# A decoder layer on one core: two more products of the MLP gates by a second Strassen level, and the context codes moved to the Mamba layer

## The chip, the cores and the metric

The kernel runs on one core of one Trainium2 chip. The metric is the device time in microseconds of one execution. Its engines are TensorE (PE), VectorE (DVE), ScalarE (ACT), GpSimd (POOL) and SyncE (SP, which here only issues transfers). Each takes its instructions in the order of the built program (which the language's scheduler settles, except where the source ties one behind another), and waits at an instruction until the semaphores that it needs have come.

## The reference

A decoder layer on x (2 x 512 tokens of 1024 numbers, float32) in three parts, each added to x:

```python
x = x + block(layernorm(x))          # Mamba-2 mixer and a gated MLP (silu(h @ gate.T) * (h @ up.T) @ down.T, 3584 wide)
q1 = fake_quant(layernorm(x)); q2 = fake_quant(ctx)     # round to 0..255 codes; ctx is 2 x 1024 x 1024
x = x + q1 @ q2
W = base + mean(abs(w - base)) * sign(w - base)         # for w1, w3 (gate, up) and w2 (down), 3584 x 1024 each
x = x + silu(h @ W1.T) * (h @ W3.T) @ W2.T              # FFN, h = layernorm(x)
```

So the FFN needs the signs of three weight differences and the mean of their absolute values, and the second part needs the codes of ctx, before either begins. The kernel makes both ahead of time, beside other work.

## The kernel before

The large products use Strassen's method in Winograd's form: seven block products in place of eight, with sums of blocks ahead and behind. The stages stand in this order on PE: the Mamba layer's projections and scan (to about 375 us), its output product, the MLP's gates, the MLP's `down` product with the quantized product between its steps, the FFN's gates, the FFN's `down`.

The function `gates` does both gate stages, name `m` for the MLP and `f` for the FFN. It loops over 14 groups of 256 rows of the gate and the up matrix, taken together. A group's seven block products are made so:

- products 1 and 2, which only appear as their sum, in `O12`. In the MLP (`two=False`), and in each stage for the groups begun early, `first_two` (L319) multiplies them plainly: 16 matmuls of 512 columns (L328), and an eviction by ACT after each four (L332). In the FFN (`two=True`) `second_level` (L763) makes them by a second level of seven products of 256 columns each (four matmuls each, L770), with left sums by `outer_left`, right sums `B12` made once by `second_level_right`, and five sums out of PSUM on DVE.
- products 6 and 7 by `second_level` in both stages (in the names the first letter is the stage, then n, the group and the bank: `mn5a` is bank a of MLP group 5; the second level of products 1 and 2 has m in place of n: `fm4a`).
- products 5, 4 and 3 plainly (`one`, L845), banks c, d and c again.

`second_level` uses bank b twice: of its seven small products the second (6) and the fifth (7) go into the same bank, and between them DVE reads it: `add(u2, p1, ps["b"])`, where p1 is a copy of bank a by ACT. `add` and `sub` are lines L187 and L190. Then come SiLU on ACT and a product on DVE (L903, L905), sums of hidden blocks (`hidden_blocks`), sums of the next group's weights (`left`), and sums of the down weights (`down_blocks`). Eight PSUM banks change sides between groups. `turn`, the sum of `O67`, is where a group's run of DVE sums begins.

Beside the gates of the MLP runs the class `Diffs` (L1101), a step at three places of each group (`side`): 34 steps in all, for w1 and w3 of each group and w2 of the last six. A step's parts stand on two engines in order: on ACT a sign into `sg` (L1147) and an absolute sum (L1148); on POOL the store of the signs (L1121), the loads of the next raw weights and base (`sw`, `smean_w`, L1116), and the subtraction (L1131). All ACT instructions of the stage are chained in the written order by `on_act`, so a sign that waits for POOL holds the evictions behind it. `sw`, `smean_w` and `sg` have two places each. At the steps in `rows`, one in each of groups 1 to 8, the place of the base is loaded with 256 rows of ctx after the subtraction (L1135); ACT (L159), DVE (L162) and ACT (L165) turn them into codes, and POOL stores them in `c2d`.

The last products of a group that are done late (`finished`, the c sum, SiLU and product of slot 3, and the sums and the store of `h`) stand in `later` in the MLP: they are issued in the next group, after two of the four steps of `first_two`.

The other half of w2 has been done in the Mamba layer by `SecondDiffs` (L343): 16 halves of 128x1024, a step at copies and activations of the projections (`at`), the subtraction on POOL (L378), sign and absolute sum on ACT (L371, L372), loads on SP (L361), stores on ACT's queue (L373).

Of the kernel before, what the change touches and what calls it, by code (L numbers as in the profile page):

```python
# [38 lines left out]
def decoder(ctx, tc, a, out):  # L39
# [273 lines left out]
    POOLS = dict(t8=1, w=2, w1=2, raw=2, ap=1, hp=1, o1=1, o12=2, o67=1, px=2, s23=1, s4=2, y12=1, y67=1, b4=2, t4=1)  # L313
# [29 lines left out]
    class SecondDiffs:  # L343

        count = 2 * W2_EARLY
# [15 lines left out]
        def step(self, at):  # L363
# [3 lines left out]
            if n:  # L367
                i, hs = self.halves(n - 1)
                w, sg = self.raw[(n - 1) % 2], self.sg[(n - 1) % 2]
                with tc.issue_after(at):  # L370
                    nc.scalar.activation(sg, w, AF.Sign)  # L371
                    nc.scalar.activation(w, w, AF.Abs, accum_out=sums[:, 2, n - 1 : n])  # L372
                nc.scalar.dma_start(signs[2][i][:, hs], sg)  # L373
            if n + 1 < self.count:
                self.load(n + 1)
            if n < self.count:
# [4 lines left out]
                )  # L381
            self.n += 1
# [380 lines left out]
    def second_level(name, banks, p1, A, B, O, between=lambda: None):  # L763
# [13 lines left out]
        on_act(lambda: nc.scalar.copy(p1, ps["a"]))  # L777
        mm("b", 6)
# [13 lines left out]
    def gates(name, act, acts, g, pl, weights, down_weight, begun, ex, two, side):  # L792
# [4 lines left out]

        act_last[:] = [] if two else [None]
# [4 lines left out]
        with g:  # L803
# [6 lines left out]
            def outer_left(i, gw, uw):  # L810

                y = pl["y12"].tile([P, 4, 2, 2, P], F32, tag="y", name=f"{name}y12_{i}")
                gv, uv = (w[:, :, :P].rearrange("p (q k) c -> p q k c", q=2) for w in (gw, uw))
                return second_level_left(gv, uv, *(y[:, j] for j in range(4)))
# [20 lines left out]
            for i in range(NG):  # L835
# [17 lines left out]
                elif not two:  # L853
                    O12, steps = first_two(name, act, pl, i, *coming[0], X)
                    for n, step in enumerate(steps):
                        if n == 2:
                            late.pop()()
                            begin = last_on(mybir.EngineType.DVE)
                        step()
                else:  # L860
                    O12 = pl["o12"].tile([P, 2, 2, L], F32, tag="o", name=f"{name}o12_{i}")
                    p1 = pl["px"].tile([P, 2, Q], F32, tag="p", name=f"{name}p12_{i}")
                    second_level(f"{name}m{i}", X, p1, A12, B12, O12)
                    add(O12[:, 1], O12[:, 0], O12[:, 1])
                if i == 0:
                    c, d = one("c", 5), one("d", 4)
                p1 = pl["px"].tile([P, 2, Q], F32, tag="p", name=f"{name}p67_{i}")
                O67 = pl["o67"].tile([P, 2, 2, L], F32, tag="o", name=f"{name}o67_{i}")
                second_level(f"{name}n{i}", Y, p1, A67, B67, O67, side or (lambda: None))
# [12 lines left out]
                if not last:  # L882
                    with tc.issue_after(turn):
                        if two and i + 1 not in begun:
                            A12 = outer_left(i + 1, *coming[0])
                        A, A67 = left(i + 1, *coming[0])
                if two and i == 0:
# [4 lines left out]
                if two and not last:  # L892
                    w2.append(down_weight(i + 1, stored))
                b, sums_to, store = w2.pop(0)
                with tc.issue_after(turn if two or not last else begin):
                    down_blocks(b, sums_to())
                store(dram[1][i])
                if not two and not last:
# [8 lines left out]
                def finished(i=i, c=c, O67=O67, h=h, last=last, product=product):  # L907
# [3 lines left out]
                    if side and not last:  # L911
                        side()
                    if last:
                        nc.sync.dma_start(dram[0][i][:, :3, :], h[:, :3, :])
                    hidden_blocks(h)
                    if last:
                        nc.sync.dma_start(dram[0][i][:, 3:, :], h[:, 3:, :])
                        return None
                    return nc.sync.dma_start(dram[0][i], h).ins
# [3 lines left out]
                if two or last:  # L923
                    stored = finished()
                else:
                    side()

                    def later(finished=finished):
                        nonlocal stored
                        stored = finished()  # L930

                    late.append(later)
# [149 lines left out]
    sgp = g.enter_context(tiles_waited(name="sgp", bufs=2))  # L1082
    pl.update(open_pools(g, "m", ("ap", "t8", "hp")))
# [4 lines left out]
    ex = halves(places[0]) + halves(places[1])  # L1088
    pl["px"] = Room(*(ex[3][:, k : k + 2 * Q].rearrange("p (a b) -> p a b", a=2) for k in (0, 2 * Q)))
    pl["o67"] = Room(places[2].rearrange("p (a b c) -> p a b c", a=2, b=2))  # L1090
    pl["y67"] = Room(places[3][:, : 3 * 4 * P].rearrange("p (a b c d) -> p a b c d", a=3, b=2, c=2))
# [8 lines left out]

    class Diffs:  # L1101
        todo = [(i, j) for i in range(NG) for j in range(3) if j < 2 or i >= W2_EARLY]
        rows = {3 + 3 * n: divmod(n, 4) for n in range(2 * TPB)}
# [6 lines left out]
        def load(self, n):  # L1110
            i, j = self.todo[n]
            self.raw[n] = []
            for tag, x in zip(("raw", "base"), FFN[j]):
                tl = pl["raw"].tile([P, KC * GW], F32, tag=tag, name=f"s{x}{i}")
                self.raw[n].append(tl)
# [7 lines left out]
        def subtract(self):  # L1123
            n = self.n
            if not n:
                self.load(0)
            self.store()
            if n + 1 < len(self.todo):
                self.load(n + 1)
            w, v = self.raw[n]  # L1130
            self.on_pool(lambda: nc.gpsimd.tensor_tensor(w, w, v, ALU.subtract))  # L1131
            if n in self.rows:
                b, i = self.rows[n]
                src = a["ctx"][b, i * 2 * P : (i + 1) * 2 * P, :].rearrange("(k p) n -> p k n", p=P)
                self.on_pool(lambda: nc.gpsimd.dma_start(v.rearrange("p (k n) -> p k n", k=2), src))  # L1135

        def step(self):
# [3 lines left out]
            w, v = self.raw.pop(self.n)  # L1141
            coded = self.rows.get(self.n)
            if coded:
                on_act(lambda: code_relu(v, v, inv["x2"], quant["x2_zp"]))
                code_round(v)
# [4 lines left out]
            if coded:  # L1150
                b, i = coded
# [287 lines left out]
```

## Time and profile before

| | |
|---|---|
| median of three runs | 2427.69 us (2424.99 to 2438.13) |
| the profiled execution | 2427.8 us, its span from first to last instruction 2425.9 us |
| mean granted TensorE clock | 0.994 |
| PE busy | 2371.1 us |
| DVE busy | 1537.4 us |
| ACT busy | 614.9 us |
| POOL busy | 413.7 us |
| MLP gates, groups 2 to 13, by PE's timeline | 566.76 to 1136.5 us |
| POOL subtractions in the MLP (L1131) | 34, 4.6 us median, 15.0 the longest |

The profile is of one execution. Its page gives the busy time of each engine, the waits, the chain of work that ended last and the costliest groups of instructions; a line number is that of the source below, and out<-in are the program's names of what is written and read. A matmul of 512 float32 columns counts as two records on PE. A timeline line gives start and duration in us, engine, line, operation, shapes, and in brackets how long the engine had been idle and what released it. A window gives busy time of each engine between two times, then the granted clock, the busy share of the DMA engines and GB/s.

### The profile page before, as it was taken

The numbers are of one execution on the slowest core, as the hardware profiler recorded it, in microseconds if no ns is written. First come the engines' busy times: TensorE is split into PE (matmuls) and PEld (weight loads), VectorE is DVE, ScalarE is ACT, GpSimd is POOL, SyncE is SP. The second block draws the span as 40 slices with busy tenths as digits, with TensorE's granted clock in tenths as the row PEclk, the third lists the DMA queues.
The fourth block names the chain that finished last, engine by engine and source line by source line (L and its number), as shares of the span: only waits on it lengthen the run. The fifth ranks groups of instructions, "written<-read, shape, count | busy, mean of one in ns | idle before, by whom it ended". The sixth has DMA issues, their size and how long they took to land.

```text
span 2425.9 us, 22738 instructions
## 1 busy us (share of the span) xinstructions
PE 2371.1 (98%) x8452; PEld 1543.4 (64%) x8452; DVE 1537.4 (63%) x2278; ACT 614.9 (25%) x784; POOL 413.7 (17%) x296
## 2 busy tenths in 40 slices
PE   7999999999999999999999999999999999999999
PEld 5445444455555555556888775667667667688888
DVE  4757677476555665665555756686776766765554
ACT  3234250334444443311000325222222222100000
POOL 1124211253554354200000011000000000000000
PEclk8999999999999999999999999999999999999999
DMA  4242241668888789756764481677577576786652
GB/s 149 96 155 88 96 147 70 199 224 330 338 356 354 304 353 374 273 190 252 247 182 140 134 238 50 180 195 213 152 199 211 152 199 196 235 261 188 196 170 65
DMA packets 182351, 494.45 MB, mean 204 GB/s; under 512 B 21216, under 2 KB 125664, under 8 KB 151264
## 3 DMA queue, kind: packets, MB, share of 16 engines
q1 hardware_dynamic: 153056, 326.26, 38.6%
q0 software_dynamic: 26880, 162.54, 22.2%
q10 hardware_dynamic: 2304, 4.20, 0.5%
q8 instruction: 67, 1.10, 0.2%
q14 instruction: 44, 0.36, 0.0%
HBM read 349.26 MB, written 145.75 MB: 204 GB/s over the span
## 4 chain that ended last, share of the span: by engine, by line
PE 75%; DMA 9%; POOL 5%; issue 3%; DVE 3%; ACT 3%; SPq 1%; POOLq 0%; ACTq 0%; DVEq 0%
DMA smean_w<-in_mean_w 4%; POOL sw L1131 4%; PE op L664 3%; PE ma L328 3%; DMA smean_w<-in_ctx 2%; SPq L959 1%; ACT sg L1147 1%; DMA m4b<-mwd 1%; PE fa L328 1%; PE dps L440 1%; PE xa L1259 1%; PE y L584 1%; ACT smean_w L159 1%; PE f1c L845 1%; PE f0c L845 1%
## 5 line engine op out<-in xcount | busy, mean ns | idle before, releaser
L1131 POOL TENSOR_TENSOR sw<-sw,smean_w 128x2048 f32<-128x2048 f32 x34 | 190.7, 5609 | 22.5 <-DMA smean_w<-in_mean_w 22.2
L1340 POOL DMA_DIRECT2D fw<-in_mean_w x42 | 36.5, 868 | 530.1 <-ACT fw L1339 479.6
L328 PE MATMUL ma<-h2T,gate_w 128*128 128x512 f32 x224 | 101.4, 595 | 8.9 <-ACT mo L332 8.9
L328 PE MATMUL ma<-h2T,up_w 128*128 128x512 f32 x224 | 102.2, 599 | 0.0
L1339 ACT ACTIVATE fw<-fpl,coeff 128x2048 f32<-128x2048 bf16 x38 | 76.2, 2005 | 91.5 <-DMA fpl<-sign 18.6
L1147 ACT ACTIVATE sg<-sw 128x2048 bf16<-128x2048 f32 x34 | 64.8, 1905 | 114.5 <-POOL sw L1131 114.5
L378 POOL TENSOR_TENSOR raw<-raw,base 128x1024 f32<-128x1024 f32 x16 | 49.9, 3116 | 191.1 <-ACT p00c L520 59.7
L328 PEld LDWEIGHTS ma<-h2T,gate_w 128*128 128x128 f32 x224 | 41.8, 190 | 61.9 <-issue 48.3
L328 PEld LDWEIGHTS ma<-h2T,up_w 128*128 128x128 f32 x224 | 43.1, 193 | 53.9 <-issue 53.9
L905 DVE TENSOR_TENSOR mh<-mpl 128x512 f32<-128x512 f32 x28 | 25.5, 911 | 80.4 <-ACT mpl L903 80.0
L903 ACT ACTIVATE fo<-fo 128x512 f32<-128x512 f32 x56 | 35.0, 626 | 137.5 <-DVE fo L187 137.5
L1148 ACT ACTIVATE sw<-sw 128x2048 f32<-128x2048 f32 x34 | 65.0, 1911 | 1.1
L664 PE MATMUL op<-wout,mz 128*128 128x512 f32 x128 | 56.6, 592 | 0.0
L1121 POOL DMA_DIRECT2D sign<-sg x34 | 19.5, 572 | 199.5 <-ACT sg L1147 199.5
L91 POOL TENSOR_TENSOR q_r<-q_e,mhalf 128x1 f32<-128x1 f32 x8 | 7.0, 876 | 249.9 <-DVE q_e L87 236.9
L332 ACT COPY mo<-ma 128x512 f32<-128x512 f32 x56 | 30.7, 579 | 72.7 <-PE ma L328 66.4
L664 PEld LDWEIGHTS op<-wout,mz 128*128 128x128 f32 x128 | 23.9, 190 | 27.7 <-issue 27.3
L190 DVE TENSOR_TENSOR mh<-mh 128x512 f32<-128x512 f32 x42 | 37.4, 891 | 1.4
L190 DVE TENSOR_TENSOR down<-down 128x512 f32<-128x512 f32 x56 | 38.1, 681 | 0.1
L905 DVE TENSOR_TENSOR fh<-fo 128x512 f32<-128x512 f32 x56 | 36.3, 684 | 1.6
L610 POOL TENSOR_TENSOR mz<-mz,ys 128x512 f32<-128x512 f32 x16 | 20.7, 1293 | 75.0 <-DVE ys L607 43.5
L159 ACT ACTIVATE smean_w<-smean_w,x_zp,inv_x 128x2048 f32<-128x2048 f32 x8 | 16.8, 2094 | 64.9 <-DMA smean_w<-in_ctx 64.9
(2078 smaller groups left out, 5628.6 us busy)
## 6 DMA issues: line engine op xcount, KB each, us to landing
fw<-in_mean_w POOLq DMA_DIRECT2D x42, 1024.0 KB, 13.6
sw<-in_w POOLq DMA_DIRECT2D x34, 1024.0 KB, 9.4
smean_w<-in_mean_w POOLq DMA_DIRECT2D x34, 1024.0 KB, 11.8
mwd<-down SPq DMA_DIRECT2D x14, 1792.0 KB, 10.6
mhd<-mh SPq DMA_DIRECT2D x13, 1792.0 KB, 8.0
fhd<-fh SPq DMA_DIRECT2D x13, 1792.0 KB, 8.1
fpl<-sign SPq DMA_DIRECT2D x38, 512.0 KB, 8.8
sign<-sg POOLq DMA_DIRECT2D x34, 512.0 KB, 6.5
```

Of the source, the lines that this page charges most:

```text
L159: return nc.scalar.activation(v, src, AF.Relu, bias=bias, scale=scale)
L190: nc.vector.tensor_tensor(out_, x, y, ALU.subtract)
L328: nc.tensor.matmul(ps[x], w[:, 4 * p + k, :P], act[0][:, 4 * p + k, :], start=not p and k == 0, stop=k == 3, skip_group_check=p > 0,)
L378: sub_ = nc.gpsimd.tensor_tensor(w, w, self.base[n % 2], ALU.subtract).ins
L664: nc.tensor.matmul(ps, A[p][:, k, t * P : t * P + P], B[p][:, k, :], start=(k == 0), stop=(k == 3))
L845: nc.tensor.matmul(into[x][j], A[j][p][:, k, :], B[p][:, k, :], start=not onto and k == 0, stop=k == 3, skip_group_check=onto,)
L905: nc.vector.tensor_tensor(h[:, slot, :], o[:, 0], o[:, 1], ALU.mult)
L1131: self.on_pool(lambda: nc.gpsimd.tensor_tensor(w, w, v, ALU.subtract))
L1147: on_act(lambda: nc.scalar.activation(sg, w, AF.Sign))
L1148: on_act(lambda: nc.scalar.activation(w, w, AF.Abs, accum_out=sums[:, j, 2 * i : 2 * i + 1]))
L1339: nc.scalar.activation(dst, src, AF.Identity, scale=coeff[:, j : j + 1])
L1340: nc.gpsimd.dma_start(dst, a[base][i].rearrange("p a b -> p (a b)"), accum_op=ALU.add)
```

## The change

- In the MLP, groups 2 to 13 make products 1 and 2 by `second_level`, as the FFN does; groups 0 and 1 still use `first_two`. The right sums `B12` are made in group 1 into a new tile `mex`, and the left sums of the next group after `left`. Their places are a new `y12` and a quarter of a spilled place (`y12_`).
- `finished` and `put` (sums and store of `h`) are separate: with `second_level`, `finished` is issued after the copy of bank a (`copied`), and `put` after the whole product.
- `Diffs` no longer loads or codes ctx. The base has one place in place of two and is loaded after the subtraction, where before it was loaded ahead of it; the signs have one place in place of two.
- `SecondDiffs` codes ctx: after a half's subtraction SP loads 128 rows of ctx into the place of the base, and the next step makes their codes (ACT, DVE, ACT) and stores them from ACT's queue, 16 times.

The diff, cut to its core:

```diff
...
             last["pe"] = last_on(mybir.EngineType.PE)
-    POOLS = dict(t8=1, w=2, w1=2, raw=2, ap=1, hp=1, o1=1, o12=2, o67=1, px=2, s23=1, s4=2, y12=1, y67=1, b4=2, t4=1)
+    POOLS = dict(t8=1, w=2, w1=2, raw=2, ap=1, hp=1, o1=1, o12=2, o67=1, px=2, s23=1, s4=2, y12=1, y67=1, ex=1, b4=2, t4=1)
     def open_pools(g, name, names, **kw):
...
                 i, hs = self.halves(n - 1)
-                w, sg = self.raw[(n - 1) % 2], self.sg[(n - 1) % 2]
+                w, v = self.raw[(n - 1) % 2], self.base[(n - 1) % 2]
+                sg, c16 = self.sg
+                b, k = divmod(n - 1, KC)
                 with tc.issue_after(at):
                     nc.scalar.activation(sg, w, AF.Sign)
-                    nc.scalar.activation(w, w, AF.Abs, accum_out=sums[:, 2, n - 1 : n])
+                    code_relu(v, v, inv["x2"], quant["x2_zp"])
+                code_round(v)
+                nc.scalar.activation(w, w, AF.Abs, accum_out=sums[:, 2, n - 1 : n])
                 nc.scalar.dma_start(signs[2][i][:, hs], sg)
+                code_out(c16, v)
+                nc.scalar.dma_start(c2d[b][:, k, :], c16)
             if n + 1 < self.count:
...
                 )
+                b, k = divmod(n, KC)
+                nc.sync.dma_start(self.base[n % 2], a["ctx"][b, k * P : (k + 1) * P, :])
             self.n += 1
...
         on_act(lambda: nc.scalar.copy(p1, ps["a"]))
+        copied()
         mm("b", 6)
...
             def outer_left(i, gw, uw):
-                y = pl["y12"].tile([P, 4, 2, 2, P], F32, tag="y", name=f"{name}y12_{i}")
                 gv, uv = (w[:, :, :P].rearrange("p (q k) c -> p q k c", q=2) for w in (gw, uw))
+                y = pl["y12"].tile([P, 2 if side else 4, 2, 2, P], F32, tag="y", name=f"{name}y12_{i}")
+                if side:
+                    s4 = pl["y12_"].tile(None, F32, "y", f"{name}y12_{i}s4")
+                    return second_level_left(gv, uv, uv[:, :, :2], y[:, 0], y[:, 1], s4)
                 return second_level_left(gv, uv, *(y[:, j] for j in range(4)))
...
                     O12 = begun[i]
-                elif not two:
+                elif i < 2:
                     O12, steps = first_two(name, act, pl, i, *coming[0], X)
...
                         if n == 2:
-                            late.pop()()
-                            begin = last_on(mybir.EngineType.DVE)
+                            for part in late:
+                                part()
                         step()
                 else:
-                    O12 = pl["o12"].tile([P, 2, 2, L], F32, tag="o", name=f"{name}o12_{i}")
+                    O12 = pl["o12" if "o12" in pl else "o1"].tile([P, 2, 2, L], F32, tag="o", name=f"{name}o12_{i}")
                     p1 = pl["px"].tile([P, 2, Q], F32, tag="p", name=f"{name}p12_{i}")
-                    second_level(f"{name}m{i}", X, p1, A12, B12, O12)
+                    first, then = late or (lambda: None, lambda: None)
+                    second_level(f"{name}m{i}", X, p1, A12, B12, O12, first)
+                    then()
                     add(O12[:, 1], O12[:, 0], O12[:, 1])
+                if late:
+                    begin = last_on(mybir.EngineType.DVE)
+                    late.clear()
                 if i == 0:
...
                 O67 = pl["o67"].tile([P, 2, 2, L], F32, tag="o", name=f"{name}o67_{i}")
-                second_level(f"{name}n{i}", Y, p1, A67, B67, O67, side or (lambda: None))
+                second_level(f"{name}n{i}", Y, p1, A67, B67, O67, between=side or (lambda: None))
                 add(O67[:, 0], O12[:, 0], O67[:, 0])
...
                     with tc.issue_after(turn):
-                        if two and i + 1 not in begun:
+                        outer = i > 0 and i + 1 not in begun
+                        if outer and not side:
                             A12 = outer_left(i + 1, *coming[0])
                         A, A67 = left(i + 1, *coming[0])
-                if two and i == 0:
+                        if outer and side:
+                            A12 = outer_left(i + 1, *coming[0])
+                if i == (1 if side else 0):
                     b = act[0].rearrange("p (q k) l -> p q k l", q=2)
...
                     coming.append(weights(i + 2, stored))
-                if two and not last:
+                if not side and not last:
                     w2.append(down_weight(i + 1, stored))
                 b, sums_to, store = w2.pop(0)
-                with tc.issue_after(turn if two or not last else begin):
+                with tc.issue_after(begin if side and last else turn):
                     down_blocks(b, sums_to())
                 store(dram[1][i])
-                if not two and not last:
+                if side and not last:
                     w2.append(down_weight(i + 1, stored))
...
                         nc.vector.tensor_tensor(h[:, slot, :], o[:, 0], o[:, 1], ALU.mult)
-                def finished(i=i, c=c, O67=O67, h=h, last=last, product=product):
+                def finished(i=i, c=c, O67=O67, product=product, more=side and not last):
                     for j in range(2):
...
                     product(3, O67[:, 0])
-                    if side and not last:
+                    if more:
                         side()
+                def put(i=i, h=h, last=last):
+                    nonlocal stored
                     if last:
...
                         nc.sync.dma_start(dram[0][i][:, 3:, :], h[:, 3:, :])
-                        return None
-                    return nc.sync.dma_start(dram[0][i], h).ins
+                    else:
+                        stored = nc.sync.dma_start(dram[0][i], h).ins
                 for slot, o in ((0, O12[:, 1]), (2, O12[:, 0]), (1, O67[:, 1])):
                     product(slot, o)
-                if two or last:
-                    stored = finished()
+                if side and not last:
+                    side()
+                    late.extend([finished, put])
                 else:
-                    side()
-                    def later(finished=finished):
-                        nonlocal stored
-                        stored = finished()
-                    late.append(later)
+                    finished()
+                    put()
         act_last.clear()
...
     pl = {**mpl, **open_pools(g, "m", ("raw",))}
-    sgp = g.enter_context(tiles_waited(name="sgp", bufs=2))
-    pl.update(open_pools(g, "m", ("ap", "t8", "hp")))
+    sgp = g.enter_context(tiles_waited(name="sgp", bufs=1))
+    pl.update(open_pools(g, "m", ("y12", "ex", "ap", "t8", "hp")))
     xd, places = spilled("m")
...
     ex = halves(places[0]) + halves(places[1])
+    more = pl["ex"].tile([P, 3, D], F32, tag="ex", name="mex")
     pl["px"] = Room(*(ex[3][:, k : k + 2 * Q].rearrange("p (a b) -> p a b", a=2) for k in (0, 2 * Q)))
     pl["o67"] = Room(places[2].rearrange("p (a b c) -> p a b c", a=2, b=2))
-    pl["y67"] = Room(places[3][:, : 3 * 4 * P].rearrange("p (a b c d) -> p a b c d", a=3, b=2, c=2))
+    y = places[3].rearrange("p (a b c d) -> p a b c d", a=4, b=2, c=2)
+    pl["y67"] = Room(y[:, :3])
+    pl["y12_"] = Room(y[:, 3])
     def mlp_down(i, after):
...
         todo = [(i, j) for i in range(NG) for j in range(3) if j < 2 or i >= W2_EARLY]
-        rows = {3 + 3 * n: divmod(n, 4) for n in range(2 * TPB)}
         raw, pool_last, unstored, n = {}, [], [], 0
...
                 self.pool_last[:] = [fn().ins]
-        def load(self, n):
-            i, j = self.todo[n]
-            self.raw[n] = []
-            for tag, x in zip(("raw", "base"), FFN[j]):
-                tl = pl["raw"].tile([P, KC * GW], F32, tag=tag, name=f"s{x}{i}")
-                self.raw[n].append(tl)
+        def load(self, n, kind):
+            if n < len(self.todo):
+                i, j = self.todo[n]
+                x = FFN[j][kind]
+                tag, bufs = (("raw", 2), ("base", 1))[kind]
+                tl = pl["raw"].tile([P, KC * GW], F32, tag=tag, bufs=bufs, name=f"s{x}{i}")
+                self.raw.setdefault(n, []).append(tl)
                 self.on_pool(lambda: nc.gpsimd.dma_start(tl, flat(a[x][i])))
...
             if not n:
-                self.load(0)
+                self.load(0, 0)
+                self.load(0, 1)
             self.store()
-            if n + 1 < len(self.todo):
-                self.load(n + 1)
+            self.load(n + 1, 0)
             w, v = self.raw[n]
             self.on_pool(lambda: nc.gpsimd.tensor_tensor(w, w, v, ALU.subtract))
-            if n in self.rows:
-                b, i = self.rows[n]
-                src = a["ctx"][b, i * 2 * P : (i + 1) * 2 * P, :].rearrange("(k p) n -> p k n", p=P)
-                self.on_pool(lambda: nc.gpsimd.dma_start(v.rearrange("p (k n) -> p k n", k=2), src))
+            self.load(n + 1, 1)
         def step(self):
...
             i, j = self.todo[self.n]
-            w, v = self.raw.pop(self.n)
-            coded = self.rows.get(self.n)
-            if coded:
-                on_act(lambda: code_relu(v, v, inv["x2"], quant["x2_zp"]))
-                code_round(v)
+            w, _ = self.raw.pop(self.n)
             sg = sgp.tile([P, KC * GW], BF16, tag="sg", name=f"sg{j}_{i}")
...
             self.unstored.append((signs[j][i], sg))
-            if coded:
-                b, i = coded
-                c16 = sgp.tile([P, KC * GW], BF16, tag="sg", name=f"cc{b}{i}")
-                on_act(lambda: code_out(c16, v))
-                to = c2d[b][:, 2 * i : 2 * i + 2, :]
-                self.unstored.append((to, c16.rearrange("p (k n) -> p k n", k=2)))
             self.n += 1
...
         "m", h2T, acts, g, pl, lambda i, after: mlp_weights[i] if i < 2 else gate_up(pl, i, after), mlp_down,
-        {0: begun_m}, ex[:3], False, diffs.step,
+        {0: begun_m}, ex[:3] + tuple(more[:, k, :] for k in range(3)), diffs.step,
     )
...
```

## The prediction

> **What bounds the kernel now.** I read the page, then the windows stage by stage, then the timelines of the single engines in one MLP group.
>
> ```profile
> span 2425.9 us, 22738 instructions
> ...
> PE 2371.1 (98%) x8452; PEld 1543.4 (64%) x8452; DVE 1537.4 (63%) x2278; ACT 614.9 (25%) x784; POOL 413.7 (17%) x296
> ```
>
> PE is busy for 98% of the span: only fewer matmul cycles, or the 54.8 us in which PE stands, can bring time. The windows of single gate groups (columns: length, then busy time of PE, PEld, DVE, ACT, POOL) say what a group costs.
>
> ```profile
> 712.32:760.22 47.90, 46.72 (x137) 25.67 (x136) 29.87 (x38) 20.69 (x21) 22.68 (x15) 1.00 0.87 332
> 904.03:950.65 46.62, 46.62 (x138) 25.91 (x137) 35.32 (x42) 20.85 (x22) 20.09 (x14) 1.00 0.92 374
> 1043.58:1090.04 46.46, 46.46 (x138) 25.76 (x137) 26.57 (x38) 5.83 (x10) 0.00 (x0) 1.00 0.46 171
> 1675.40:1720.30 44.90, 44.90 (x162) 30.28 (x161) 31.34 (x47) 10.70 (x12) 2.60 (x3) 1.00 0.66 186
> ```
>
> These are MLP group 5 (with context codes), 9 (signs, no codes), 12 (neither) and FFN group 4, which already has what the change gives the MLP. So 46.5 us is the MLP's PE work, 44.9 us that of the new form, and group 5 has 1.2 us of PE idle on top. Where that comes from stands in PE's timeline, and the new form's deadline too:
>
> ```profile
> 720.52 3.70 PE L328 MATMUL ma<-h2T,gate_w 128*128 128x512 f32 x8 [1.18 <-ACT mo L332]
> ...
> 1675.36 1.89 PE L770 MATMUL fm4a<-x3T,fw 128*128 128x256 f32 x8
> ...
> 1682.27 1.89 PE L770 MATMUL fm4b<-fpl,fy 128*128 128x256 f32 x8
> ```
>
> The first line: PE waits for an eviction on ACT. The other two: the second use of bank b starts 6.9 us after the group does; before it DVE must have read the bank (the sum u2). ACT was late because its sign waited for POOL, and POOL for DVE:
>
> ```profile
> 716.05 1.91 ACT L1147 ACTIVATE sg<-sw 128x2048 bf16<-128x2048 f32 x1 [8.01 <-POOL sw L1131]
> ```
> ```profile
> 708.64 7.38 POOL L1131 TENSOR_TENSOR sw<-sw,smean_w 128x2048 f32<-128x2048 f32 x1
> ...
> 934.50 5.04 POOL L1131 TENSOR_TENSOR sw<-sw,smean_w 128x2048 f32<-128x2048 f32 x1 [0.20 <-DMA smean_w<-in_mean_w]
> ```
> ```profile
> 711.56 0.68 DVE L187 TENSOR_TENSOR mpl<-mpl,m4c 128x512 f32<-128x512 f32 x1
> ...
> 935.09 5.00 DVE L190 TENSOR_TENSOR mu10s<-up_w 128x512 f32<-128x512 f32 x1
> ```
>
> POOL's subtraction takes 4.5 us undisturbed. Issued at 708.64 while DVE ran sums with both inputs in SBUF, it got going only when DVE came to a sum that reads PSUM (711.56), and ended 4.5 us after that. Once it runs, the next SBUF sum of DVE is held until it ends (935.09: 5.00 us instead of 0.68), while sums from PSUM run on (one at 736.33 took 0.69 inside a subtraction). So each of the three subtractions of a group can cost DVE 4.4 us.
>
> **The change part by part.** All against the profiled execution: 2427.8 us, span 2425.9; the median of the runs, 2427.69, is the same.
>
> *Matmuls.* Groups 2 to 13 replace 16 matmuls of 512 columns (32 rows in the trace, 13.73 us) by 28 of 256 (fm4a to fm4c, 12.13 us by their starts). By whole periods, from which nothing is left out, 46.54 (the mean of groups 9 and 12) less 44.86 (fm4a to fm5a, 1675.36 to 1720.22) is 1.68 us, times 12: **-20.2**. It lies on PE, the bound.
>
> *Stalls that go.* Groups 2 to 8 last from 566.76 to 904.03 (PE's timeline), 337.3 us; 7 x 46.54 is 325.8. The rest, **-11.5**, is PE waiting for L332's copies behind signs that the context codes had delayed (the codes: 2.09 + 1.99 us on ACT, 1.23 on DVE, a load of 8.0 us on POOL's queue, once in each of groups 1 to 8). Codes and copies both leave.
>
> *What is late next.* The new form needs DVE 10 more sums a group (31.3 against 26.6 us in the windows), and u2 within 6.9 us. In FFN group 3 DVE begins the run of sums after n at 1655.75 and reaches the first c sum at 1674.39, 18.6 us later; the next group starts 19.6 us after 1655.75. With one subtraction inside the run (+4.3, from 5.00 - 0.68) the c sum starts 3.3 us into the next group. By then the next subtraction has been asked for: the second step's sign and absolute sum stand behind the SiLU of the first d sum. In group 9 that sum began 14.5 us after the run (930.88 to 945.42, a subtraction inside); the run begins 44.9 - 19.6 = 25.3 us into a group, and with 0.7 for the sum and 0.6 for the SiLU the sign begins at 41. Sign and absolute sum take 3.9, the next issue on POOL 1: asked for 1 us into the next group. As at 708.64 it gets going at the c sum and ends 3.3 + 4.5 = 7.8 us into the group. The product of the new `finished`, an SBUF operation, stands ahead of u2 on DVE and is held until then; u2 ends at 7.8 + 0.6 + 0.7 = 9.1. PE wanted it at 6.9, so 2.2 us stall. It happens at each boundary with a third step: 34 steps, two in group 0 and three in each later one, make boundaries 2 to 11. Between nothing (subtraction after the product) and 4.4 us (held twice) I take 2.0: 10 x 2.0 = **+20**.
>
> *Single buffers.* With one place for bases, the load of base n+1 is queued on POOL after subtraction n, and POOL's next subtraction waits for its landing; behind that waits stand the sign on ACT and all of ACT's later copies. The nearest row is the context load, issued at the same place of the queue:
>
> ```profile
> smean_w<-in_mean_w POOLq DMA_DIRECT2D x22, 1024.0 KB, 11.8
> ...
> smean_w<-in_ctx POOLq DMA_DIRECT2D x8, 1024.0 KB, 8.0
> ```
>
> A step then takes at least 4.5 + 0.5 + 8.0 = 13.0 us, three 39, under the period of 46.9: hidden, with some 8 us to spare. With 11.8 us (today's base, which lands behind the raw load issued with it) three steps take 50.4, and the cover is gone. I take 8.0, because the raw load will be issued about 5 us ahead: 0. One place for signs: a store lands 6.7 us after its issue, inside the 13 us of a step: 0.
>
> The Trainium skill (DMA: Bandwidth & Descriptors, Anatomy of one DMA — SWDGE path) gives 2.0 us plus bytes over 436 GB/s, so an estimate of 4.4 us for this megabyte. The rows show 8.0 and 11.8, with other queues at work. By the page three steps would take 28 us and no rival on this side would be left; the trace decides.
>
> *B12.* Four 128x1024 sums in group 1, 1.23 us each, stand on DVE between hidden sums and the u2 of n1. From 0 to 5; most of it beside the two products there: **+1**.
>
> *Mamba layer.* 16 times: 1.05 us twice on ACT, 0.69 on DVE (a 128x1024 rounding, the row of the queries), a 512 KB load on SP after the POOL subtraction, a store on ACT's queue. SP's waits for subtractions put the w_in loads behind them; three places for w_in leave a whole tile (24 us) of slack. The reloads of x (`hid`) stand behind the last context load, which is issued at about 306 us, before their places are free. ACT and DVE are 33% and 65% busy in the first 440 us, and PE hardly stands. It bites where PE already waits for these two: 80 to 105 us (idle 3.4 us; DVE 17.95 of 20 busy), 255 to 260, and 330 to 336. One rounding or ReLU there is 0.7 to 1.1 us. Below nothing is excluded, as only work is added; above, every rounding on the path is 11 us. Near the low end: **+2**.
>
> *Elsewhere.* POOL's queue loses 8 loads and 8 stores in the MLP, DMA 12 MB. The FFN's group loop keeps its order; the `down` stage loads the same places. 0, give or take 3.
>
> Sum: -20.2 - 11.5 + 20 + 1 + 2 = -8.7, so **2419 us**.
>
> **Rivals.** *No clash (2399).* If the third subtraction comes after the product of `finished` (its base lands later than 4 us into the group), DVE is not held and the 20 us don't arise: 2419 - 20. For: landing times scatter from 5.3 to 16.8 us, so some boundaries will be spared. Against: the request is due 3 us before.
> *The base load sets the pace (2472).* If it lands in 11.8 us, a step takes 16.8, with 0.6 for waits on DVE 17.4; three take 52.2, and ten groups run at that instead of 46.9: +53. It decides from a landing of 10 us (3 x 15.6 = 46.9). For: DMA is 87 to 92% busy in groups 5 and 9, and would be about as full. Against: the context load, in the same place, took 8.0 with more in flight.
> *Mamba pays in full (2428).* All 16 roundings on the path: +9 more. Against: no PE idle from 107 to 255 us.
> *That the change does not do what it says* can be left aside: the order of the built program has 28 products of 256 columns in each of MLP groups 2 to 13 where it had 16 of 512.
>
> **How the numbers follow.** Forecast (stalls of 1 to 3 us a boundary, 2409 to 2429 by itself) 0.44, no clash 0.36, base load 0.15, Mamba 0.05. About 0.5%, 12 us, is what a measurement of this kernel tells from no change. Faster by more needs under 2415.6: no clash and a sliver of the forecast, 0.38. Slower by more, over 2439.8: the base load and a sliver, 0.17. Within: 0.45. The range goes from 2397 (no clash, nothing paid elsewhere) to 2440 (stalls of 4 us, costs at their upper half), and leaves out the base load.
>
> **What would show it.** Right: MLP groups 2 to 11 at 46 to 48 us, 12 and 13 at 44.9; PE idle before the second mm b, released by DVE; a long product (over 4 us) on DVE beside a subtraction 3 to 8 us into the group. Wrong: groups at 44.9 throughout (no clash), or signs on ACT waiting for POOL while POOL waits for the base's DMA, with groups of 50 us and more. Mamba: out_product starting over 5 us later would put that term wrong.

## The result, and the profile after

The changed kernel takes 2445.4 us (median of nine), before 2426.3 beside it: ratio 1.0077, 95% interval 1.0057 to 1.0097. It is slower by 19 us, where 2419 was forecast. One of the nine executions took 9699 us and is left out of the ratio. The profiled execution took 2444.3 us, with a span 16.6 us longer than before's. Its page:

```profile
span 2442.5 us, 23439 instructions
...
PE 2364.9 (97%) x8732; PEld 1604.9 (66%) x8740; DVE 1685.3 (69%) x2410; ACT 607.9 (25%) x776; POOL 397.6 (16%) x280
```

The matmul work removed is 20 us, yet PE's busy time fell by 6 only (from 2371.1): some matmuls ran longer. PE's timeline, cut at the same landmarks in both kernels, says where the 16.6 us arose:

| stretch | before | after | difference |
|---|---|---|---|
| start to the first matmul of MLP group 0 | 464.63 | 469.44 | +4.8 |
| groups 0 and 1 | 102.13 | 105.33 | +3.2 |
| groups 2 to 13 | 569.58 | 578.15 | +8.6 |
| `down`, quantized product, FFN | 1289.56 | 1289.58 | 0.0 |

Windows of MLP group 3, group 5 and group 12 (the first without a third step), and of 3.4 us inside group 3; columns as before, the number ahead of the last two being the granted clock:

```profile
624.25:673.48 49.23, 46.80 (x161) 31.38 (x160) 40.51 (x48) 16.29 (x18) 20.69 (x12) 0.97 0.78 299
721.63:769.90 48.27, 45.48 (x162) 30.07 (x160) 42.86 (x48) 16.29 (x18) 20.68 (x12) 1.00 0.81 305
1062.98:1108.06 45.08, 45.08 (x161) 30.23 (x160) 33.19 (x48) 4.66 (x8) 0.00 (x0) 1.00 0.35 122
633.75:637.15 3.40, 3.40 (x8) 2.77 (x9) 2.63 (x4) 2.75 (x3) 0.76 (x2) 0.50 0.92 316
```

Group 12 has the 45 us of the new form; groups 2 to 11 last 48.2 to 49.5. The start of group 3 in the timeline of all engines shows the announced chain:

```profile
625.79 6.76 POOL L1152 TENSOR_TENSOR sw<-sw,smean_w 128x2048 f32<-128x2048 f32 x1
...
628.10 1.27 DVE L187 TENSOR_TENSOR mpl<-mpl,m2c 128x512 f32<-128x512 f32 x2
...
629.47 3.63 DVE L925 TENSOR_TENSOR mh<-mpl 128x512 f32<-128x512 f32 x1
...
633.02 0.67 DVE L187 TENSOR_TENSOR mo<-mpl,mm3b 128x512 f32<-128x512 f32 x1
...
633.75 3.67 PE L779 MATMUL mm3b<-mex,my 128*128 128x256 f32 x8 [2.43 <-DVE mo L187]
```

POOL's subtraction is issued 1.5 us into the group, gets going at the c sums (628.10) and ends 4.5 us after; the product of `finished` is held meanwhile (3.63 us in place of 0.68); u2 comes at 633.02; PE idles 2.43 us before the second use of bank b. Then the line says one thing more: these eight records take 3.67 us where the same eight take 1.89 elsewhere. PE's clock was halved for 3.4 us (the last window above, 0.50).

### The profile page after: what moved, and what is told of

Same layout as the page of the kernel before. It is cut to its first block, busy times and chain, and to the rows that moved or that the text cites. A ratio compares the mean times of both kernels' runs of the same rounds, so it can differ in the third digit from the quotient of the medians.

```text
span 2442.5 us, 23439 instructions
## 1 busy us (share of the span) xinstructions
PE 2364.9 (97%) x8732; PEld 1604.9 (66%) x8740; DVE 1685.3 (69%) x2410; ACT 607.9 (25%) x776; POOL 397.6 (16%) x280
## 4 chain that ended last, share of the span: by engine, by line
PE 74%; DVE 15%; issue 4%; DMA 3%; SPq 2%; ACT 1%; POOL 1%; DVEq 0%; POOLq 0%; ACTq 0%
PE op L673 3%; DVE mh L925 2%; DVE mpl L187 2%; SPq L978 2%; DVE acc L543 1%; DVE down L190 1%; DVE mo L187 1%; PE ma L328 1%; PE dps L449 1%; DVE mpl L190 1%; PE fa L328 1%; PE m0c L857 1%; PE f1c L857 1%; PE f0c L857 1%; PE f11c L857 1%
## 5 line engine op out<-in xcount | busy, mean ns | idle before, releaser
L1347 ACT ACTIVATE fw<-fpl,coeff 128x2048 f32<-128x2048 bf16 x38 | 76.2, 2004 | 92.7 <-DMA fpl<-sign 20.1
L385 POOL TENSOR_TENSOR raw<-raw,base 128x1024 f32<-128x1024 f32 x16 | 42.4, 2649 | 207.3 <-DMA base<-in_mean_w 61.1
L1161 ACT ACTIVATE sg<-sw 128x2048 bf16<-128x2048 f32 x34 | 64.8, 1906 | 34.7 <-POOL sw L1152 34.7
L925 DVE TENSOR_TENSOR mh<-mpl 128x512 f32<-128x512 f32 x28 | 51.5, 1840 | 5.6 <-ACT mpl L923 4.4
L923 ACT ACTIVATE mpl<-mpl 128x512 f32<-128x512 f32 x28 | 17.7, 631 | 115.5 <-DVE mpl L187 115.4
L187 DVE TENSOR_TENSOR mo<-mo 128x1024 f32<-128x1024 f32 x12 | 36.3, 3028 | 1.3
L923 ACT ACTIVATE mo<-mo 128x512 f32<-128x512 f32 x28 | 17.5, 624 | 73.8 <-DVE mo L187 73.8
L187 DVE TENSOR_TENSOR hid<-hid,op 128x512 f32<-128x512 f32 x24 | 15.9, 683 | 24.0 <-PE op L673 24.0
L619 POOL TENSOR_TENSOR mz<-mz,ys 128x512 f32<-128x512 f32 x16 | 20.7, 1294 | 65.9 <-DVE ys L616 44.8
L328 PE MATMUL fa<-x3T,fw 128*128 128x512 f32 x64 | 28.7, 595 | 2.1 <-ACT fo L332 2.1
L118 PE MATMUL h1T<-ident,h 128*128 128x128 f32 x64 | 13.4, 361 | 17.6 <-ACT h L440 10.8
L190 DVE TENSOR_TENSOR fh<-fh 128x512 f32<-128x512 f32 x42 | 29.0, 690 | 1.0
```

Of the source, the lines that this page charges most:

```text
L187: nc.vector.tensor_tensor(out_, x, y, ALU.add)
L190: nc.vector.tensor_tensor(out_, x, y, ALU.subtract)
L328: nc.tensor.matmul(ps[x], w[:, 4 * p + k, :P], act[0][:, 4 * p + k, :], start=not p and k == 0, stop=k == 3, skip_group_check=p > 0,)
L923: on_act(lambda: nc.scalar.activation(o[:, 0], o[:, 0], AF.Silu))
L925: nc.vector.tensor_tensor(h[:, slot, :], o[:, 0], o[:, 1], ALU.mult)
L1161: on_act(lambda: nc.scalar.activation(sg, w, AF.Sign))
```

## Experiments

Ratios are against the kernel before, run on the same chip in the same comparison (2427 to 2429 us). The theory: a sum of DVE with both inputs in SBUF is held for as long as a POOL subtraction runs, and the second level has put such sums ahead of sums that PE waits for. The rival: DVE simply has too much to do at the boundary.

**Subtraction cut to 64 columns in the MLP** (changed kernel):

```diff
-            self.on_pool(lambda: nc.gpsimd.tensor_tensor(w, w, v, ALU.subtract))
+            self.on_pool(lambda: nc.gpsimd.tensor_tensor(w[:, :64], w[:, :64], v[:, :64], ALU.subtract))
```

> The changed kernel with the MLP's POOL subtraction cut to 64 of 2048 columns (the rest of the difference is left out; loads, signs, absolute sums, waits and order stay). Theory (a sum with both inputs in SBUF is held while POOL subtracts): the product of finished takes 0.7 us in place of 3.6, u2 is in time, no halved clock, groups 2 to 11 last 44.9 to 45.1 us, and the stall of 4.2 us behind group 0 goes too; 2445.4 - 39 - 5 = 2401 us. Rival (DVE has too much to do at the boundary, whatever POOL does): groups stay at 48 to 49 us, 2440 to 2445 us.

Measured 2401.6 us, ratio 0.9879 (0.9857 to 0.9901). Groups 2 to 11 last 44.86 us each, the stall behind group 0 is gone, and the product in group 3 takes its own time and waits for its SiLU instead:

```profile
619.62 0.69 DVE L925 TENSOR_TENSOR mh<-mpl 128x512 f32<-128x512 f32 x1 [2.19 <-ACT mpl L923]
```

DVE has the same sums to do and is in time. The rival falls; what the second level lost in the gates, POOL's subtractions took. Whether by holding DVE or by keeping ACT's signs waiting this run can't say, since both go; the reordered kernels below do.

**Subtraction as two instructions** of 1024 columns:

```diff
+            for k in (0, D):
+                self.on_pool(lambda: nc.gpsimd.tensor_tensor(w[:, k : k + D], w[:, k : k + D], v[:, k : k + D], ALU.subtract))
```

> The changed kernel with each POOL subtraction of the MLP as two instructions of 1024 columns. Theory in its simple form (DVE is held until the POOL instruction ends): the product is held for one half of 2.3 us, u2 ends some 7.4 us into the group and PE idles 0.3 to 0.5 us there, too short for the clock to drop; groups of 45.3 to 46.3 us, 2407 to 2420 us. If the second half begins before the held product gets its turn, nothing changes: 2445 us. Rival (DVE is too full): 2445 us.

Measured 2432.8 us, ratio 1.0015 (1.0001 to 1.0029): better than the change by some 15 us, but short of what was expected. DVE and PE at the start of group 3 (620.02):

```profile
625.39 1.47 DVE L925 TENSOR_TENSOR mh<-mpl 128x512 f32<-128x512 f32 x1
626.78 0.67 DVE L187 TENSOR_TENSOR mo<-mpl,mm3b 128x512 f32<-128x512 f32 x1
627.38 2.24 DVE L190 TENSOR_TENSOR mh<-mh 128x512 f32<-128x512 f32 x1
...
627.51 1.99 PE L779 MATMUL mm3b<-mex,my 128*128 128x256 f32 x8 [0.41 <-DVE mo L187]
...
633.17 1.99 PE L779 MATMUL mm3c<-h2T,mpl 128*128 128x256 f32 x8 [1.94 <-DVE mo L187]
```

The product got its turn between the halves and the stall at bank b fell to 0.41, as the theory has it. But the second half then held the first hidden sum (2.24), which stands ahead of u3, and PE waited 1.94 us at bank c instead. Of the Trainium skill, SBUF — State Buffer (SBUF: two separate sides) says that a GpSimd operation and a DVE operation with two SBUF inputs exclude each other for whole instructions; these lines agree: each half held one sum, to its end. That DVE gets a turn between the halves is not the rule, though: eight weight sums of this run were held through both halves and took 5.6 us in place of 0.7.

**The held product moved behind c22** (the computation unchanged; the same sums in another order on DVE; `ins` is the sum that the product is queued behind):

```diff
         on_act(lambda: nc.scalar.copy(p1, ps["a"]))
-        copied()
         mm("b", 6)
...
-        add(c22, u3, ps["c"])
+        copied(nc.vector.tensor_tensor(c22, u3, ps["c"], ALU.add).ins)
...
-                    product(3, O67[:, 0])
+                    product(3, O67[:, 0], ins)
```

> The changed kernel with the product of finished queued on DVE behind c22 of the second level (it stood ahead of u2); the c sums and the subtraction stay where they were. Theory (the held product is what makes u2 late): u2, u3 and c22 read PSUM and run on during the subtraction, PE has no idle before the second mm b, groups 2 to 11 last 45 to 46 us, no halved clock there; 2445.4 - 30 to - 38, so 2407 to 2415 us. Rival (DVE is too full): u2 comes only the product's own 0.7 us earlier, 1.7 us of idle stay, 2430 to 2438 us.

Measured 2419.8 us, ratio 0.9952 (0.9934 to 0.9969): the chain is cut, and the result is already faster than before, though short of the 2407 to 2415 us expected. No second mm b waits any more. Seven groups last 44.86, five 46.60, as the windows of groups 3 and 4 show:

```profile
620.88:667.48 46.60, 45.13 (x162) 30.15 (x160) 38.78 (x47) 16.07 (x17) 21.65 (x12) 1.00 0.83 312
667.48:712.34 44.86, 44.86 (x162) 30.24 (x161) 35.04 (x48) 16.19 (x19) 20.96 (x12) 1.00 0.84 328
```

In group 3 the next subtraction, begun 14.3 us into the group when its base had landed, held the last hidden sum, ahead of u2 of n, and PE waited:

```profile
635.20 5.16 POOL L1151 TENSOR_TENSOR sw<-sw,smean_w 128x2048 f32<-128x2048 f32 x1 [2.06 <-DMA smean_w<-in_mean_w]
635.90 5.00 DVE L190 TENSOR_TENSOR mh<-mh 128x512 f32<-128x512 f32 x1
640.82 0.67 DVE L187 TENSOR_TENSOR mpl<-mpl,mn3b 128x512 f32<-128x512 f32 x1
...
641.55 1.99 PE L779 MATMUL mn3b<-mpl,mpl 128*128 128x256 f32 x8 [1.47 <-DVE mpl L187]
```

In group 4 the base landed 1.6 us later in the group, and the hidden sum was through.

**All sums seen held moved** behind the ones PE waits for (the last hidden sum behind u2 of n, the 128x1024 sum behind c22 of n, and in group 0 the weight sums behind the d sums; in these lines `end()` is the last hidden sum and its `ins` u2 of n, the `ins` of the other is c22 of n):

```diff
+                free = turn if i or not side else last_on(mybir.EngineType.DVE)
                 if not last:
-                    with tc.issue_after(turn):
+                    with tc.issue_after(free):
...
+                        with tc.issue_after(ins) if ins else nullcontext():
+                            end()
...
+                        with tc.issue_after(ins):
+                            add(O12[:, 1], O12[:, 0], O12[:, 1])
```

> The kernel of the late product, with every other DVE sum that was seen held ahead of a sum PE waits for queued behind that sum: the last hidden sum behind u2 of n, the 128x1024 sum of the first two products behind c22 of n, and in group 0 the sums of the next weights and of the down weights behind the d sums. Theory (held sums are the whole loss of the gates): no PE idle in MLP groups 0 to 13 but the old 1.7 us in group 1, groups 2 to 13 last 44.9 us; from 2419.8, 5 x 1.74 less for the groups and 5 less behind group 0: 2406 us. Rival (the holding only moves on, to u3 and c22 of n): groups of 46 to 47 us remain, 2413 to 2420 us.

Measured 2406.9 us, ratio 0.9916 (0.9897 to 0.9935). Groups 2 to 13 last 44.9 us each. Subtractions hold sums as before, but none that PE needs soon. ACT's signs wait even longer for POOL than in the changed kernel (46.5 us in all, there 34.7), so those waits were not the loss. PE still idles 1.0 and 1.2 us in group 1. Part is given back: the gates end 25.8 us earlier than before, the execution 20.1, since in `down` PE now idles 4.2 us for operands of its second product. That was not followed up.

**The codes alone** (kernel before, `SecondDiffs` of the change, `Diffs` without ctx and otherwise as before):

> The kernel before with one part of the change alone: the context codes are made in the Mamba layer; the MLP keeps the plain first two products, two places for bases and for signs, and its old order of loads. Theory (codes and second level are separate terms): the output product starts about 4.8 us later, as in the changed kernel, the stalls of 11.5 us in MLP groups 2 to 8 go, groups 2 to 8 last 46.6 us each; 2426.3 + 4.8 - 11.5 = 2419.6 us. Rival (the old stalls came from the subtractions themselves, not from the codes): groups 2 to 8 stay at 48 us, 2431 us.

Measured 2417.9 us, ratio 0.9951 (0.9934 to 0.9969). The rival falls: groups 2 to 13 take 46.46 us each. In the profiled execution they are 12.0 us shorter together (11.5 forecast) and group 0 starts 3.8 us later (4.8 forecast); another 3 us, in groups 0 and 1 and behind the gates, was not forecast, so the gain is nearer 11 us than the 7 of the sum.

**The codes, with one place for bases and one for signs** (`Diffs` as in the change, plain first two products):

> The kernel of the codes alone (plain first two products in the MLP), with one place for bases and one for signs and the base loaded after the subtraction, as in the changed kernel. Prediction's term: 0, so 2417.9 us as with the codes alone. Rival (the load's place in POOL's queue is what sets off the clash behind group 0, and the base's landing delays subtractions into evictions): the 4.2 us stall behind group 0 appears, 4 to 8 us more, 2422 to 2426 us.

Measured 2423.8 us, ratio 0.9982 (0.9972 to 0.9992), 0.3% more than the codes alone. POOL and DVE behind group 0, with one place:

```profile
520.90 0.54 POOL L1125 DMA_DIRECT2D sw<-in_w  x1 [1.54 <-ACT sw L1150]
521.03 5.49 DVE L190 TENSOR_TENSOR mg1s<-gate_w 128x512 f32<-128x512 f32 x1
...
521.45 4.51 POOL L1140 TENSOR_TENSOR sw<-sw,smean_w 128x2048 f32<-128x2048 f32 x1
...
527.17 3.78 PE L854 MATMUL m0c<-h2T,mg0s 128*128 128x512 f32 x4 [4.23 <-DVE mo L187]
```

and with two places (the codes alone):

```profile
516.38 0.68 DVE L190 TENSOR_TENSOR mg1s<-gate_w 128x512 f32<-128x512 f32 x1
...
516.86 0.54 POOL L1125 DMA_DIRECT2D smean_w<-in_mean_w  x1
516.98 1.28 DVE L187 TENSOR_TENSOR mo<-mpl,m0c 128x512 f32<-128x512 f32 x2
517.41 4.54 POOL L1140 TENSOR_TENSOR sw<-sw,smean_w 128x2048 f32<-128x2048 f32 x1
```

With two places POOL issues the base's load first, 0.5 us, and by then DVE is at a c sum, which reads PSUM. Without that load the subtraction catches the weight sum ahead of it, and PE stands 4.23 us.

**The Mamba layer.** Three kernels, all sums of the MLP moved in the first two: the subtraction of `SecondDiffs` cut to 64 columns, the rounding of the codes cut to 64 columns, and the kernel before with the subtraction cut.

```diff
-                sub_ = nc.gpsimd.tensor_tensor(w, w, self.base[n % 2], ALU.subtract).ins
+                sub_ = nc.gpsimd.tensor_tensor(w[:, :64], w[:, :64], self.base[n % 2][:, :64], ALU.subtract).ins
...
-                code_round(v)
+                code_round(v[:, :64])
```

> The kernel with all sums moved, and the POOL subtraction of the Mamba layer cut to 64 of 1024 columns (the rest of that difference is left out). Theory (the Mamba layer's loss is the same holding: the base, loaded later, puts the subtraction beside the convolution's sums): from the first p00u transpose or product to the first transpose of h2T 350 us or less, where before it was 350.1 and in the changed kernel 355.4; 5 us or more less than the kernel with all sums moved, about 2400 us. Rival (the added codes on DVE and ACT themselves): 355 us, less than 1 us of difference.

> The kernel with all sums moved, and the rounding of the codes in the Mamba layer cut to 64 of 1024 columns (the rest of the rounding is left out, all waits stay). Theory of the holding: from p00u to h2T still 354 to 355 us, less than 1.5 us of difference. Rival (the added work on DVE): 351 us, 4 us less than the kernel with all sums moved.

> The kernel before, with the POOL subtraction of the Mamba layer cut to 64 of 1024 columns (the rest of that difference is left out), to see what the holding cost there before the change. Theory (holding is the Mamba layer's whole loss in both kernels, the codes themselves cost nothing on the path): the first transpose of h2T at 436 to 437 us as in the changed kernel with the same cut, so 4 to 5 us less than before, about 2423 us. Rival (the codes cost something of their own): h2T at 433 us or earlier, 2419 us.

Measured 2397.2 (0.9874, 0.9857 to 0.9892), 2406.6 (0.9911, 0.9894 to 0.9927) and 2419.8 us (0.9969, 0.9954 to 0.9984). So the subtraction costs this layer about 10 us after the change, and some 8 before; ACT is not seen waiting for it there, so the cost is put down to holding. The third kernel came out at its rival's 2419 us, not the theory's 2423. The starts of h2T named in the expectations were too coarse to read: the beginning of the execution alone (up to p01a) scatters from 43.1 to 49.3 us over the profiles. From p01a's first matmul to that of group 0 PE takes 418.5 us before and 424.0 after; 424.3 with all sums moved, 414.5 with the subtraction cut as well, 421.0 with the rounding cut; 411.4 with the subtraction cut in the kernel before. A stretch of halved clock that begins between 330 and 341 us and costs 1.7 us is in all of these but the last two. Without it, holding cost 5.5 us before and 9.8 after, and with the subtraction cut the codes themselves cost 1.4: of the layer's 5.5 us more, about 4 are holding. These are single profiles; the medians' intervals don't resolve the 4. The groups of costliest instructions between 60 and 345 us (six sums of one convolution; busy, mean ns) show where it comes from, before:

```profile
L534 DVE SCALAR_TENSOR_TENSOR acc<-p10u,convw,acc 128x511 f32<-128x511 f32 (+2 forms) x6 | 4.0, 740 | 0.0
```

after:

```profile
L385 POOL TENSOR_TENSOR raw<-raw,base 128x1024 f32<-128x1024 f32 x16 | 42.4, 2649 | 207.3 <-DMA base<-in_mean_w 61.1 <-ACT p00c L529 59.3 <-ACT mz L534 19.9
...
L543 DVE SCALAR_TENSOR_TENSOR acc<-p10u,convw,acc 128x511 f32<-128x511 f32 (+2 forms) x6 | 6.3, 1085 | 0.0
```

A sum held makes 6.3 of 4.0 us. Of twelve such lines one has it before, four after. Before, the subtractions in question held sums of weights instead (2.2 us in place of 0.7): the base, whose place is now lent to ctx, is loaded later, POOL waits for it (61.1 us; before, this wait ended on ACT), and the subtraction slips into the convolution. Over the whole layer the held operations of DVE are nearly as many before (12, together 20.7 us over their usual time) as after (14, 24.4 us); so it is which sum is held, more than how many, that PE feels.

**The Mamba layer's subtraction on DVE** (all sums of the MLP moved; the tie to the step's activation stays in this kernel, though its expectation says that it goes):

```diff
-                sub_ = nc.gpsimd.tensor_tensor(w, w, self.base[n % 2], ALU.subtract).ins
+                sub_ = nc.vector.tensor_tensor(w, w, self.base[n % 2], ALU.subtract).ins
```

> The kernel with all sums moved, and the subtraction of the Mamba layer made by DVE (16 of 128x1024, about 1.2 us each), without the tie to the step's activation. If DVE is never held there by POOL and the bases land in time: h2T up to 8 us earlier, 2398 to 2403 us. Rival (DVE now waits itself for bases that land late, and the convolution behind them): h2T later, 2410 to 2430 us.

Measured 2391.6 us, ratio 0.9856 (0.9838 to 0.9875): beats both kernels, by 36 us the kernel before. Sixteen sums more on DVE cost less than sixteen on POOL that hold it:

```profile
L385 DVE TENSOR_TENSOR raw<-raw,base 128x1024 f32<-128x1024 f32 x16 | 19.5, 1222 | 20.3 <-DMA base<-in_mean_w 9.5 <-ACT mz L534 3.1 <-ACT p02c L529 1.9
```

## Why the prediction was wrong

The mechanism it chose is the one that happened; its terms, against the profiled executions:

| term | predicted | measured |
|---|---|---|
| matmuls and stalls that go | -31.7 | -31.3 (569.58 less 12 x 44.86) |
| stalls at boundaries 2 to 11 | +20 | +39.6 (their ten periods 488.2, less 448.6) |
| groups 0 and 1 (B12 +1, single buffers 0) | +1 | +3.2 |
| Mamba layer | +2 | +4.8 |
| elsewhere | 0 | +0.3 |

- *Matmuls, stalls that go:* right, to half a microsecond. With the subtraction cut to 64 columns the groups last 44.86, and the codes alone gave the gain forecast for them in the groups (12.0 us for 11.5).
- *What is late next:* the steps to u2 are right, nearly to the time (subtraction asked for at 1 us, seen at 1.5; u2's end at 9.1, seen at 9.4). The step that failed is the size, "I take 2.0: 10 x 2.0"; 4.0 was measured, the mean of ten boundaries, none of them spared. It has three parts. The second mm b starts 2.6 us late. The delay goes on through u3 and c22, to 3.3 us at the end of m (the four boundaries at 48.2); the sum stopped at the first bank. And at six of the ten PE came back at half its clock, 1.65 us lost, after which the wait at bank c vanishes: 4.4 a boundary in all. The prediction showed four windows with a granted clock of 1.00, and never asked what an idle of 2.2 us does to it: the term for the clock was nothing, without a reason. The profile of before could have told:

```profile
470.67:473.67 3.00, 3.00 (x11) 1.97 (x12) 1.44 (x3) 2.06 (x4) 1.67 (x3) 0.59 1.03 193
577.51:580.51 3.00, 3.00 (x7) 1.44 (x8) 1.94 (x3) 0.96 (x2) 1.83 (x3) 1.00 0.92 324
```

  These are the 3 us after a wait of 2.44 and one of 2.43 us: one came back at a mean clock of 0.59, the other at full speed. The last section shows what makes the difference.
- *Single buffers, 0:* the reason was right and the term wrong. The base lands in 5.8 us (median), a step is hidden, signs on ACT wait for POOL 35 us in all where it was 115, and the rival "base load sets the pace" did not occur. The estimate from the Trainium skill (DMA: Bandwidth & Descriptors, Anatomy of one DMA — SWDGE (gpsimd) path; 4.4 us) was nearer than the row the prediction sided with (8.0). But a load that no longer stands ahead of a subtraction also lets the subtraction start 0.5 us earlier, and that puts it on the wrong sum behind group 0: 0.3% by the run with one place. B12's own +1 is not to be seen: with the subtraction cut, groups 0 and 1 last 99.8 us, with the codes alone and no B12 100.6.
- *Mamba, +2:* about right for the codes (1.4). Missed was the move of the subtraction by a base that waits for the codes: the prediction followed the new loads on SP, and not what POOL's later start meets on DVE.
- *The range* ended at 2440: stalls of 4 us (+20) and 1 us for all the rest. Most of the Mamba layer's loss and group 0's had the same cause as the boundaries, so the three rose together. "No clash" was given 0.36 because landings scatter; at every boundary the base had landed before the request, so the scatter spared none.

By the runs, as ratios: the codes -0.5%, the single places +0.3%, the second level with its order +1.0%, the last only in this order. With the sums moved the second level brings in groups 2 to 13 what it promised (538.3 us, where the codes alone have 557.6; 20.2 was forecast), and `down` gives some of it back.

## What to carry to other kernels

In these runs a POOL operation on two tiles acts as a lock on DVE's two-input SBUF sums: for each, look at which sum DVE has next when it starts, and what PE waits for behind that sum. Queue the sums that read PSUM ahead of the ones that can be held, or give the work to DVE where it has the time. A change that moves a load by half a microsecond moves that meeting point, so it belongs in the sum even where the load itself is hidden; and a PE idle of about 2 us or more is to be priced with the clock that may follow.

## What the runs showed of the hardware

PE's clock after short idles. A halved stretch lasts 3.4 us and costs 1.7. It followed 6 of the 10 boundary idles of 2.4 to 2.7 us of the changed kernel, otherwise alike; 2 of the 10 where an idle of 0.4 us at most and one of 1.4 to 1.9 us came 5.7 us apart (the two halves); none of the five of 1.47 us with the product moved. What decides is the phase. In each of the twelve profiles every change of the granted clock lies on a grid of 3.413 us, and a step of that grid is halved when PE stood long enough in the step before it. Two neighbouring steps each of groups 3 and 4 of the changed kernel, the first with the start of the idle (columns as before):

```profile
630.34:633.75 3.41, 0.98 (x5) 0.53 (x3) 3.41 (x3) 1.17 (x1) 2.78 (x2) 1.00 0.95 408
633.76:637.17 3.41, 3.41 (x8) 2.78 (x9) 2.62 (x4) 2.74 (x3) 0.78 (x2) 0.50 0.93 317
678.13:681.54 3.41, 2.42 (x12) 1.79 (x10) 3.31 (x2) 0.52 (x1) 3.41 (x1) 1.00 1.05 426
681.55:684.96 3.41, 1.98 (x9) 1.78 (x10) 3.34 (x5) 3.12 (x2) 1.33 (x3) 1.00 0.86 311
```

In group 3 the whole idle of 2.43 us lies in one step, and the next is halved; in group 4 the grid cuts it into 0.99 and 1.43, and nothing follows. So at all ten: the six that were halved had 1.98 to 2.43 us in one step, the four others 1.80 at most. Over the twelve profiles, between 60 and 2370 us, a halved step followed each of the 41 full-speed steps with more than 1.95 us of idle and none of some 8000 with less than 1.74; of the 14 between, four. The Trainium skill (TensorE: Matmul & The Clock Gate, Part 1: The HAM clock gate) describes a free-running window of 3.4 us and names idle gaps above that as the ones that halve the clock: the window agrees with the grid, the threshold doesn't, some 1.9 us within one step was enough here.

The holding lasts until the POOL instruction ends: a subtraction of 128x2048 made one DVE sum of 0.68 us take up to 5.5. A sum that reads PSUM passes: of the 213 in the gates of the changed kernel none took over 0.69 us, and 33 of them ran inside a subtraction. Sums of two SBUF tiles are not the only ones held. In the run with the rounding cut, what is left of a rounding (one tile in, 64 columns, 0.18 us as a rule) took 2.35 us beside a subtraction:

```profile
293.84 4.22 POOL L385 TENSOR_TENSOR raw<-raw,base 128x1024 f32<-128x1024 f32 x1 [7.62 <-DMA base<-in_mean_w]
295.77 2.35 DVE L162 TENSOR_SCALAR base<-base 128x64 f32<-128x64 f32 x1
```
